# Two attention blocks on one core: a second Strassen step for four of the seven products of layer 0's second Q and K

## The chip, the cores and the metric

One NeuronCore of a Trainium2 chip runs the whole program. TensorE (PE) multiplies, VectorE (DVE) and ScalarE (ACT) empty its accumulators (PSUM banks) and do the element work, GpSimd (POOL) does a few small operations, and SyncE (SP) issues the DMAs. Each engine works through its own queue in order; semaphores join the queues. The metric is the device time of one execution in microseconds (us).

## The reference

x is 8 samples of 512 channels and 32x32 positions, float32 throughout. Two blocks follow each other, each with a residual. Cut to what matters, with C = 512 and N = 1024 positions:

```python
# layer 0, 8 heads of 64 channels
h = group_norm(x)                                  # 32 groups of 16 channels
q, k, v = split(qkv_w @ h + qkv_b)                 # three 512x512 products over N positions
o = softmax(q.T @ k / 8) applied to v, head by head
x = x + proj_w @ o + proj_b
# layer 1, one head over all channels, norm over the whole sample
n = norm(x)
q, k, v = wq @ n + bq, wk @ n + bk, wv @ n + bv
x = x + wo @ attention(q, k, v) + bo
```

## The kernel before

The kernel goes through the samples b = 0 to 7 one after the other. For one sample the stages are: layer 0's V (`make_v`, L517), its second Q and K (`pairs_qk` with oc = 1), the attention (64 units of scores, exponential and values), the first Q and K of the next sample (`pairs_qk` with oc = 0), the projection, and layer 1. "First" Q and K are output channels 0 to 127 and 256 to 383 (chunks 0 and 2), "second" are chunks 1 and 3. The attention goes through the chunks in the order 0, 2, 1, 3, so it begins with what the earlier stage has made.

Nearly all products are made by Strassen's scheme in Winograd's form (`strassen`, L410): both factors are cut into 2x2 quarters, and seven products A11 B11, A12 B21, S1 T1, S2 T2, S3 T3, A22 T4 and S4 B22 take the place of eight, where S1 to S4 and T1 to T4 are sums and differences of quarters. The weights' sums are made once by the first sample and stored in DRAM (`Weight`, L195); every later sample loads the finished set of seven parts (1792 KB) through SP. The sums T of the activations are made by VectorE (`Combined`, L378).

In the second Q and K, a quarter of the weight is 256 channels in by 128 out (parts of Q and of K apart), a quarter of the activations 256 channels by 512 positions. So one product is two matmuls (k = 0, 1) of 128x128 weights on 512 columns, four PE instructions in float32. Q and K are two `strassen` groups, and `together` (L454) lets them take turns. A group has two banks: `line`, in which A11 B11, S2 T2, S3 T3 and A22 T4 pile up, and `single` for the others. A bank may be written again only when ScalarE or VectorE has read it. ScalarE copies the line after its first three products (L421); VectorE adds a copy, the bias and a bank together (`done`, L511), and ScalarE writes the fourth quarter (L509).

`at_steps` (L466) walks through the steps of a stage and calls hooks between them. With PE, ACT and DVE the order in which the code calls is the order of their queues (`manual_schedule`); SP's order is found by the framework. In the second Q and K the hooks are: step 4 the mean of the next sample's group norm, step 5 its variance (small matmuls by `in_group`, L285, whose result VectorE takes, L289; GpSimd raises it to the power -0.5, L335; VectorE makes scale and shift, L342 to L344), steps 6 and 7 the normed x (L368 on ScalarE, L370 on VectorE), steps 8 and 9 the sums T for the next sample (L396) and the first two scores.

PSUM is one pool with two tags, "s" and "o", and two buffers of two banks for each. `room` (L278) gives the statistics a spare half of an "o" buffer when `strassen` has noted one in `spares`, and else a new "s" buffer. In the attention a unit is one chunk, one half of the queries and 128 keys: scores into an "s" buffer (L716), exponential by ScalarE (L645), a running sum of the exponentials by VectorE (L647), and values into an "o" buffer (L735). After a chunk's 16 units its running sums are folded by DMAs (`fold`, L824) and joined (L836). All tiles of 128x1024 in SBUF (x, q, k, v, exponentials, sums) come from one pool of 36 buffers, tag "t" (L88).

Layer 1 has a second Strassen step already: `halve_a` and `halve_b` (L1028, L1039) make the sums of a product's quarters, and `twice` (L1127) makes the product of 256 columns at a time in seven steps, with a line bank and a single bank.

Of the kernel before, what the change touches and what calls it, by code (L numbers as in the profile page):

```python
# [37 lines left out]
FP = mybir.dt.float32  # L38
AF = mybir.ActivationFunctionType
ALU = mybir.AluOpType  # L40
# [6 lines left out]
P = 128  # L47
# [4 lines left out]
HALF = 512  # L52
HD = 64
# [7 lines left out]
V_NW0, V_NB0, V_BQ0, V_BK0, V_BV0, V_BP0 = (NC * i for i in range(6))  # L61
# [4 lines left out]
def two_attention_blocks(  # L66
# [17 lines left out]
    nc = tc.nc  # L84
    B = x.shape[0]
# [4 lines left out]
    dram = ctx.enter_context(tc.tile_pool(name="dram", bufs=1, space=bass.MemoryType.DRAM))  # L90
# [47 lines left out]
    vec = const.tile([P, 12 * NC], FP, tag="vec", name="vec")  # L138
# [54 lines left out]
    stored = {}  # L193

    class Weight:  # L195
# [104 lines left out]
    class Norm:  # L300
# [54 lines left out]
        def bias(self):  # L355
            both, bias = self.tile("both"), self.tile("bias", NC)
            nc.vector.tensor_tensor(both, self.mean, self.rstd, ALU.mult)
            nc.vector.tensor_scalar(bias, made["v_g"], both, None, ALU.mult)
            nc.vector.tensor_tensor(bias, made["v_b"], bias, ALU.subtract)
            return bias  # L360
# [17 lines left out]
    class Combined:  # L378
# [5 lines left out]
        def take(self, quarters):  # L384
            (b11, self.b12), (b21, b22) = quarters
            for i in range(1, 5):
                self.parts[f"T{i}"] = tile2(f"t{i}_{self.name}")
            self.parts.update(B11=b11, B21=b21, B22=b22)
# [21 lines left out]
    def strassen(multiply, done, name, width=HALF, us=None, end=None):  # L410
# [36 lines left out]
            done(0, 1, single, us[2])  # L447
        yield

    def in_turn(*groups):  # L450
        for g in groups:
            yield from g

    def together(*groups):  # L454

        groups = list(groups)
        spares.clear()
        while groups:
            for g in list(groups):
                if next(g, g) is g:  # L460
                    groups.remove(g)
                else:
# [54 lines left out]
    def make_v(w, n2, bs, vs, name):  # L517


        def pairs(t):  # L520
            return t.rearrange("p (u o) -> p u o", u=2)

        def done(i, half, bank, u):
            v = vs[2 * half + n2][:, :, i * 2 * P : (i + 1) * 2 * P]
            if u is None:
                nc.scalar.copy(v, pairs(bank))
            else:
                nc.vector.tensor_tensor(v, pairs(bank), pairs(u), ALU.add)  # L528

        return strassen(by_positions(w, n2, bs), done, f"{name}_{n2}")  # L530
# [13 lines left out]
    class Rows:  # L544
# [33 lines left out]
        def add(self, i, name):  # L578

            t, c = const.tile([P, NC], FP, tag=name, name=name), self.columns[:, i]  # L580
            nc.vector.tensor_tensor(c[:, :2, :], c[:, :2, :], c[:, 2:, :], ALU.add)
            nc.vector.tensor_tensor(t, c[:, 0, :], c[:, 1, :], ALU.add)
            made[name] = t
            return t
# [90 lines left out]
    def flat(t):  # L675
        return t.rearrange("p h n -> p (h n)")

    def pairs_qk(w, oc, bs, qs, ks, b):

        for ts, n, bias, name in [(qs, 0, V_BQ0, "q"), (ks, 1, V_BK0, "k")]:  # L680
            for i in (oc, oc + 2):
                ts[i] = tile2(f"{name}_0_{b}_{i}")
            yield make_channels(
                w.parts[n], 0, oc, bs, vec[:, bias : bias + NC],
                lambda chunk, half, ts=ts: ts[chunk][:, half, :], f"{name}_0_{b}",
            )

    ORDER = [0, 2, 1, 3]

    def layer0(bs, qs, ks, b, norm_next):  # L690
# [3 lines left out]
        w = next_weight().parts[0]  # L694
        hooks = {}
        if norm_next is not None:
            for n in range(NC):
                hooks[n + 4] = [lambda cc=n, half=half: norm_next.of_half(cc, half) for half in range(2)]
            hooks[8] = [lambda cc=cc: norm_next.of_channels(cc) for cc in range(NC)]
        at_steps(together(*[make_v(w, n2, bs, vs, f"v_0_{b}") for n2 in range(2)]), hooks)  # L700
        vs = [vs[nt // 2][:, nt % 2, :] for nt in range(NT)]
        if b == 0:
            for rows in throughs:
# [4 lines left out]
        quarters = [(slice(i * HD, (i + 1) * HD), slice(j * HD, (j + 1) * HD), i, j)  # L708
                    for i in range(2) for j in range(2)]

        def scores(pair, g, kt):
            name = f"0_{b}_{pair}_{g}_{kt}"
            s = banks("s", f"s_{name}")
            for rows, cols, j, half in quarters:
                k0 = kt * P + half * HD
                nc.tensor.matmul(  # L716
                    s[cols, j, :], flat(ks[pair])[rows, k0 : k0 + HD],
                    qs[pair][rows, g, :], start=True, stop=True,
                )
            if kt == 1:  # L720
                first, accs[pair, g] = accs[pair, g], tile2(f"acc_{name}")
            else:
                first = accs.get((pair, g))
            p = exponentials(s, HD**-0.5, accs.get((pair, g)), first, name)
            if kt == 0:
                accs[pair, g] = p
            return p
# [35 lines left out]
        w = next_weight()  # L763
# [10 lines left out]
        hooks = {8: [lambda: score(0)], 9: [lambda: score(1)]}  # L774
# [9 lines left out]
        if b == 0:  # L784
            hooks.setdefault(7, []).append(p0.finish)
            hooks[8].insert(0, bias0)
        at_steps(together(*pairs_qk(w, 1, bs, qs, ks, b)), hooks)
        xs = load_x(b, nc.sync)
        norm = norm1(xs, b)

# [108 lines left out]
        for i in range(2, len(units) + 2):  # L899
# [6 lines left out]
            pair, g, kt = units[i - 5] if i >= 5 else (None, None, None)  # L906
# [92 lines left out]
    def attention1(xs, norm, b, at_values):  # L999
# [14 lines left out]
        bs = combine.parts  # L1014
# [1 line left out]

        twice_a, twice_b = {}, {}

        def halve(part, order):

            quarter = {}
            for i in range(2):
                for j in range(2):
                    k, n = order(i, j)
                    quarter[f"{i + 1}{j + 1}"] = part[:, k, n * 2 * P : (n + 1) * 2 * P]
            return quarter

        def halve_a(name):  # L1028
            q = {f"A{n}": v for n, v in halve(q_parts[name], lambda i, j: (j, i)).items()}
            t = flat(tile2(f"{name}_twice_{b}"))  # L1030
            q.update({f"S{n + 1}": t[:, n * 2 * P : (n + 1) * 2 * P] for n in range(4)})
            for n, x, y, op in [
                (1, "A21", "A22", ALU.add), (2, "S1", "A11", ALU.subtract),
                (3, "A11", "A21", ALU.subtract), (4, "A12", "S2", ALU.subtract),
            ]:
                nc.vector.tensor_tensor(q[f"S{n}"], q[x], q[y], op)
            twice_a[name] = q

        def halve_b(name):  # L1039
            q = {f"B{n}": v for n, v in halve(bs[name], lambda i, j: (i, j)).items()}  # L1040
            t = flat(tile2(f"{name}_twice_{b}"))
            q.update({f"T{n + 1}": t[:, n * 2 * P : (n + 1) * 2 * P] for n in range(4)})
            for n, x, y in [(1, "B12", "B11"), (2, "B22", "T1"), (3, "B22", "B12"), (4, "B21", "T2")]:
                nc.vector.tensor_tensor(q[f"T{n}"], q[x], q[y], ALU.subtract)
            twice_b[name] = q

        def make_q(c):
            def done(i, half, bank, u):
# [62 lines left out]
        def line(t):  # L1111


            bank = banks("s", f"ps_s_1_{b}_{t}")[:, 0, :]
            for a, v, to in [
                ("A11", "B11", ps[0][t // 2][0]), ("S2", "T2", ps[1][t // 2][0]),
                ("S3", "T3", ps[0][t // 2][1]),
            ]:
                for k in range(2):
                    nc.tensor.matmul(  # L1120
                        bank, bs[v][:, k, t * P : (t + 1) * P], q_parts[a][:, k, :],
                        start=a == "A11" and k == 0, stop=k == 1, skip_group_check=True,
                    )
                nc.scalar.copy(to[:, t % 2, :], bank)  # L1124
                yield
# [721 lines left out]
```

## Time and profile before

| | |
|---|---|
| median of 3 runs | 2872.4 us (2872.23 to 2872.4) |
| the profiled execution, its own time | 2871.3 us |
| its span, first to last instruction | 2869.6 us |
| granted TensorE clock | 1.0 |
| V of sample 3 (1119.66 to 1143.67) | 24.0 us; DVE busy 13.0, ACT 4.7 |
| second Q and K of sample 3, to the second scores (1143.67 to 1169.46) | 25.8 us |
| attention of sample 2 (816.6 to 926.9) | 110.3 us; PE busy throughout, DVE 86.7, ACT 70.2 |
| x, 512 KB a load, from issue to landing | 7.2 us (median of 92) |
| HBM read, written | 137.43 MB, 28.57 MB |

The profile page gives busy time by engine, the chain of work that ended last, and groups of instructions by source line. Timelines list instructions in order: start, duration, engine, line, operation, what is written from what, how many; in brackets the idle time before, and what ended it. PE's ends are modelled and overlap the next start, so the pace of PE is read from starts.

### The profile page before, as it was taken

How to read it: one execution, taken by the hardware profiler on the slowest of the kernel's cores; microseconds unless marked ns; L12 is line 12 of the kernel's file. 1: busy time of each engine (PE TensorE's matmuls, PEld its weight loads, DVE VectorE, ACT ScalarE, POOL GpSimd, SP SyncE). 2: the span in 40 equal slices, each digit the busy share in tenths (PEclk: the TensorE clock that was granted, in tenths of full speed). 3: DMA queues.
4: the chain of work that ended last, by engine and by line, in shares of the span. 5: the costliest groups of instructions: out<-in, count | busy, mean ns of one | idle time of the engine just before them, and what ended most of it. 6: DMA issues, size and time to landing. Idle time of an engine off the chain costs nothing.

```text
span 2869.6 us, 35809 instructions
## 1 busy us (share of the span) xinstructions
PE 2861.8 (100%) x14480; PEld 1436.3 (50%) x14480; DVE 1934.8 (67%) x2524; ACT 1110.3 (39%) x1536; POOL 109.5 (4%) x84
## 2 busy tenths in 40 slices
PE   9999999999999999999999999999999999999999
PEld 5434754347533475334653356533565335553365
DVE  5686576865757657676666766677665776647857
ACT  3462324623156231552315523165232652326432
POOL 0000000000000010000100001000010000100001
PEclk9999999999999999999999999999999999999999
DMA  8412122121222213212032120321203222122001
GB/s 272 162 41 73 52 95 92 42 74 52 95 92 49 75 43 110 82 45 92 26 121 73 44 91 26 121 78 46 84 26 121 78 56 78 38 80 68 8 1 38
DMA packets 77661, 210.87 MB, mean 73 GB/s; under 512 B 19888, under 2 KB 20656, under 8 KB 71088
## 3 DMA queue, kind: packets, MB, share of 16 engines
q1 hardware_dynamic: 77344, 208.48, 22.7%
q8 instruction: 115, 1.88, 0.3%
q14 instruction: 58, 0.48, 0.1%
q10 hardware_dynamic: 144, 0.02, 0.0%
HBM read 137.43 MB, written 28.57 MB: 58 GB/s over the span
## 4 chain that ended last, share of the span: by engine, by line
PE 98%; DVE 1%; SPq 0%; DMA 0%; issue 0%; ACT 0%; DVEq 0%; ACTq 0%
PE s L716 15%; PE ps_o L735 15%; PE ps_v L494 13%; PE ps_q L479 13%; PE ps_o L1244 13%; PE ps_k L479 7%; PE ps_p L479 6%; PE ps_s L1120 6%; PE ps_l L1136 4%; PE ps_s L1136 3%; PE ps_wvo L596 0%; PE ps_wqk L626 0%; DVE inv L658 0%; PE ps_o L1301 0%; DVE acc L647 0%; PE ps_sum L844 0%
## 5 line engine op out<-in xcount | busy, mean ns | idle before, releaser
L645 ACT ACTIVATE p<-s 128x1024 f32<-128x1024 f32 x512 | 523.9, 1025 | 322.2 <-PE s L716 310.5
L647 DVE TENSOR_TENSOR acc<-acc,p 128x1024 f32<-128x1024 f32 x384 | 469.0, 1221 | 103.4 <-ACT p L645 91.5
L716 PE MATMUL s<-q,k 64*64 64x512 f32 x4096 | 531.5, 590 | 0.0
L735 PE MATMUL ps_o<-p,v 64*64 64x512 f32 x4096 | 528.7, 589 | 0.0
L716 PEld LDWEIGHTS s<-q,k 64*64 64x64 f32 x4096 | 154.0, 133 | 288.9 <-issue 266.0
L735 PEld LDWEIGHTS ps_o<-p,v 64*64 64x64 f32 x4096 | 156.6, 133 | 282.8 <-issue 278.0
L528 DVE TENSOR_TENSOR v<-ps_v,u_v 128x512 f32<-128x512 f32 x96 | 66.2, 689 | 164.0 <-PE ps_v L494 111.4
L421 ACT COPY u_v<-ps_v 128x512 f32<-128x512 f32 x96 | 56.3, 586 | 303.5 <-PE ps_v L494 294.8
L1244 PE MATMUL ps_o<-t_p,s_v 128*128 128x512 f32 x384 | 168.2, 594 | 0.0
L421 ACT COPY u_q<-ps_q 128x512 f32<-128x512 f32 x96 | 55.9, 582 | 250.0 <-PE ps_q L479 250.0
L647 DVE TENSOR_TENSOR acc<-p,p 128x1024 f32<-128x1024 f32 x64 | 77.8, 1216 | 84.3 <-ACT p L645 84.3
L1146 DVE TENSOR_TENSOR p<-ps_l,p 128x512 f32<-128x512 f32 x104 | 71.1, 690 | 82.0 <-PE ps_l L1136 82.0
L1120 PE MATMUL ps_s<-s_q,t 128*128 128x512 f32 x256 | 120.3, 592 | 0.0
L1244 PEld LDWEIGHTS ps_o<-t_p,s_v 128*128 128x128 f32 x384 | 72.3, 190 | 94.5 <-issue 87.5
L1109 ACT ACTIVATE p<-p,factor 128x512 f32<-128x512 f32 (+1 forms) x112 | 86.8, 782 | 77.4 <-DVE p L1146 50.2
L479 PE MATMUL ps_q<-t,w_wqk 128*128 128x512 f32 x256 | 116.0, 597 | 0.0
L479 PE MATMUL ps_p<-t_p,w_p 128*128 128x512 f32 x256 | 114.3, 596 | 0.7 <-DVE inv L658 0.6
L494 PE MATMUL ps_v<-w_wvo,t 128*128 128x256 f32 x512 | 113.1, 379 | 0.0
L1244 PE MATMUL ps_o<-p,v 128*128 128x512 f32 x256 | 111.8, 594 | 0.1
L1146 DVE TENSOR_TENSOR p<-ps_s,p 128x512 f32<-128x512 f32 x88 | 60.7, 689 | 75.0 <-PE ps_s L1136 74.2
L856 DVE RECIPROCAL inv<-inv 128x512 f32<-128x512 f32 x28 | 93.7, 3346 | 22.9 <-ACT inv L654 22.9
L1124 ACT COPY p<-ps_s 128x512 f32<-128x512 f32 x96 | 56.1, 584 | 125.6 <-PE ps_s L1120 124.5
(320 smaller groups left out, 4083.9 us busy)
## 6 DMA issues: line engine op xcount, KB each, us to landing
x<-in_x SPq DMA_DIRECT2D x92, 512.0 KB, 7.2
w_qk<-stored_qk SPq DMA_DIRECT2D x14, 1792.0 KB, 7.2
inv<-inv SPq DMA_DIRECT2D x248, 64.0 KB, 2.0
w_wqk<-stored_wqk SPq DMA_DIRECT2D x8, 1792.0 KB, 8.1
fold<-acc SPq DMA_DIRECT2D x56, 256.0 KB, 3.1
w_wvo<-stored_wvo SPq DMA_DIRECT2D x8, 1792.0 KB, 7.7
out<-x SPq DMA_DIRECT2D x28, 512.0 KB, 2.8
w_v<-stored_v SPq DMA_DIRECT2D x7, 1792.0 KB, 7.1
```

The costliest lines, as they stand in the source:

```text
L421: nc.scalar.copy(us[n][:, :width], line[:, :width])
L479: nc.tensor.matmul(bank, w[a][:, k, c * P : (c + 1) * P], bs[b][:, k, :], start=fresh and k == 0, stop=k == 1, skip_group_check=True,)
L494: nc.tensor.matmul(bank[:, u * 2 * P : (u + 1) * 2 * P], bs[b][:, k, n * P : (n + 1) * P], w[a][:, k, :], start=fresh and u == k == 0, sto ...
L645: nc.scalar.activation(p, s, AF.Exp, scale=factor)
L647: nc.vector.tensor_tensor(acc, first, p, ALU.add)
L716: nc.tensor.matmul(s[cols, j, :], flat(ks[pair])[rows, k0 : k0 + HD], qs[pair][rows, g, :], start=True, stop=True,)
L735: nc.tensor.matmul(o[cols, half, :], vs[kt][rows, c0 : c0 + HD], p[rows, j, :], start=kt == 0, stop=kt == NT - 1,)
L856: nc.vector.reciprocal(invs[g], invs[g])
L1120: nc.tensor.matmul(bank, bs[v][:, k, t * P : (t + 1) * P], q_parts[a][:, k, :], start=a == "A11" and k == 0, stop=k == 1, skip_group_check ...
L1136: nc.tensor.matmul(bank[:, u * 2 * P : (u + 1) * 2 * P], v[y][:, u * P : (u + 1) * P], a[x], start=start and u == 0, stop=True, skip_group ...
L1146: nc.vector.tensor_tensor(at(r, t), bank, at(r, t), ALU.add)
L1244: nc.tensor.matmul(bank, v_parts[kt // 2][a][:, kt % 2, c * P : (c + 1) * P], p_parts[kt // 2][b][:, kt % 2, cols], start=fresh and kt == ...
```

## The change

Samples 1 to 7 make the second Q and K by `pairs_qk_twice`; sample 0 keeps `pairs_qk`. Q's and K's 128 output channels are now taken as the two block rows of one 256x256 weight. Four products (A12 B21, S1 T1, S4 B22, A22 T4) take a second step: each is cut again into 2x2 blocks, of 128x128 weights and 128 channels by 256 positions, and made as seven products of one matmul of 256 columns. Two of the four go together: their blocks lie side by side in one bank, are read by one instruction, and go to one tile (`c11` holds the first output half's C11 and C22, `c12` C12 and C21). `pair(0)` and `pair(1)` take turns over 14 steps; then `line(0)` for Q and `line(1)` for K make A11 B11, S2 T2 and S3 T3 in one step as before, over 6 steps, and VectorE adds the line and the bias into the tiles after each product. The hooks of steps 4 to 9 become those of steps 14 to 19.

The sums of the activations' quarters (T1 to T4 of B21, T1, B22 and T4) are made by VectorE in the first four steps of V: 16 subtractions of 128x256 a sample, into four new tiles. The sums of the weights' quarters (16 of 128x128) are made once, after the second scores of sample 0, and stored in DRAM (two stores of 512 KB); each later sample loads them (two loads) before its V, into two more tiles. q and k of these chunks now lie as halves in `c11` and `c12`, and the scores index them so. Layer 1's `halve_a` and `halve_b` call the new shared `sums_a` and `quarters_b`, and do what they did.

```diff
+    def sums_a(q, t):
+
+        n = t.shape[1] // 4
+        q.update({f"S{i + 1}": t[:, i * n : (i + 1) * n] for i in range(4)})
+        for i, x, y, op in [
+            (1, "A21", "A22", ALU.add), (2, "S1", "A11", ALU.subtract),
+            (3, "A11", "A21", ALU.subtract), (4, "A12", "S2", ALU.subtract),
+        ]:
+            nc.vector.tensor_tensor(q[f"S{i}"], q[x], q[y], op)
+        return q
...
+    def quarters_b(part, name):
+
+        q = {f"B{n}": v for n, v in halve(part, lambda i, j: (i, j)).items()}
+        t = flat(tile2(name))
+        q.update({f"T{n + 1}": t[:, n * 2 * P : (n + 1) * 2 * P] for n in range(4)})
+        for n, x, y in [(1, "B12", "B11"), (2, "B22", "T1"), (3, "B22", "B12"), (4, "B21", "T2")]:
+            nc.vector.tensor_tensor(q[f"T{n}"], q[x], q[y], ALU.subtract)
+        return q
...
+    PAIRS = [[("A12", "B21"), ("S1", "T1")], [("S4", "B22"), ("A22", "T4")]]
+
+    class WeightTwice:
...
+        def __init__(self, name, make=None):
+            tiles = [flat(tile2(f"{name}_twice_{n}")) for n in range(2)]
+            key, self.tiles = f"{name}_twice", tiles
+            if make is None:
+                nc.sync.dma_start(tiles[0], stored[key][:, : 8 * P])
+                nc.sync.dma_start(tiles[1], stored[key][:, 8 * P :])
+                return
+            for n, pair in enumerate(PAIRS):
+                for i, (a, _) in enumerate(pair):
+                    sums_a(self.quarters(a, make), tiles[n][:, i * 4 * P : (i + 1) * 4 * P])
+            stored[key] = dram.tile([P, 16 * P], FP, tag=key, name=f"stored_{key}")
+            for n in range(2):
+                nc.sync.dma_start(stored[key][:, n * 8 * P : (n + 1) * 8 * P], tiles[n])
...
+    def by_two_steps(rows_of, twice_a, bs, twice_b, pairs, bias, name):
+
+        def pair(n):
+            line, single = (banks(tag, f"ps_{tag}{n}_{name}")[:, 0, :] for tag in "so")
+
+            def multiply(bank, x, y, start):
+                for i, (a, v) in enumerate(PAIRS[n]):
+                    nc.tensor.matmul(
+                        bank[:, i * 2 * P : (i + 1) * 2 * P], twice_a[a][x], twice_b[v][y],
+                        start=start and i == 0, stop=True, skip_group_check=True,
+                    )
+
+            def at(r, t):
+                return pairs[n][r][:, :, t * 2 * P : (t + 1) * 2 * P]
+
+            def of(bank):
+                return bank.rearrange("p (i q) -> p i q", i=2)
+
+            def add(bank, r, t):
+                nc.vector.tensor_tensor(at(r, t), of(bank), at(r, t), ALU.add)
+
+            def take(bank, r, t):
+                nc.scalar.copy(at(r, t), of(bank))
+
+            for bank, x, y, start, use, r, t in [
+                (line, "A11", "B11", True, take, 0, 0), (single, "A12", "B21", True, add, 0, 0),
+                (line, "S2", "T2", False, take, 0, 1), (single, "S1", "T1", True, take, 1, 1),
+                (line, "S3", "T3", False, add, 1, 1), (single, "S4", "B22", False, add, 0, 1),
+                (line, "A22", "T4", False, take, 1, 0),
+            ]:
+                multiply(bank, x, y, start)
+                use(bank, r, t)
+                yield
+
+        def line(i):
+            bank = banks("o", f"ps_l{i}_{name}")[:, 0, :]
+
+            def multiply(a, v, start):
+                for k in range(2):
+                    nc.tensor.matmul(
+                        bank, rows_of(i, a)[:, k, :], bs[v][:, k, :], start=start and k == 0,
+                        stop=k == 1, skip_group_check=True,
+                    )
+
+            def add(j, half, n):
+                c = pairs[j][i][:, half, :]
+                nc.vector.scalar_tensor_tensor(c, bank, bias(i, n), c, ALU.add, ALU.add)
+
+            (c11, c22), (c12, _) = ([p[i][:, half, :] for half in range(2)] for p in pairs)
+            nc.vector.tensor_tensor(c12, c12, c22, ALU.add)
+            multiply("A11", "B11", True)
+            add(0, 0, 0)
+            yield
+            multiply("S2", "T2", False)
+            add(1, 0, 0)
+            yield
+            multiply("S3", "T3", False)
+            add(0, 1, 1)
+            add(1, 1, 1)
+            yield
+
+        yield from together(pair(0), pair(1))
+        yield from together(line(0), line(1))
...
+    def pairs_qk_twice(w, twice_a, oc, bs, twice_b, qs, ks, b):
+
+        pairs = [[tile2(f"{n}_{name}_0_{b}_{oc}") for name in "qk"] for n in ["c11", "c12"]]
+        for i, ts in enumerate([qs, ks]):
+            (c11, c22), (c12, c21) = ([p[i][:, half, :] for half in range(2)] for p in pairs)
+            ts[oc], ts[oc + 2] = [c11, c12], [c21, c22]
+
+        def bias(i, n):
+            at = [V_BQ0, V_BK0][i] + oc + 2 * n
+            return vec[:, at : at + 1]
+
+        of = both_of(w)
+        return by_two_steps(of, twice_a.all(of), bs, twice_b, pairs, bias, f"qk_0_{b}")
...
+        twice_b = {}
+        if b > 0:
+            twice_a = WeightTwice("qk13")
+            for n, part in enumerate(["B21", "T1", "B22", "T4"]):
+                hooks.setdefault(n, []).append(lambda part=part: twice_b.update(
+                    {part: quarters_b(bs[part], f"{part}_twice_0_{b}")}
+                ))
...
-                    s[cols, j, :], flat(ks[pair])[rows, k0 : k0 + HD],
-                    qs[pair][rows, g, :], start=True, stop=True,
+                    s[cols, j, :], ks[pair][k0 // HALF][rows, k0 % HALF : k0 % HALF + HD],
+                    qs[pair][g][rows, :], start=True, stop=True,
...
-        at_steps(together(*pairs_qk(w, 1, bs, qs, ks, b)), hooks)
+        if b == 0:
+            hooks[9].append(lambda: WeightTwice("qk13", both_of(w)))
+            at_steps(together(*pairs_qk(w, 1, bs, qs, ks, b)), hooks)
+        else:
+            hooks = {n + 10: more for n, more in hooks.items()}
+            at_steps(pairs_qk_twice(w, twice_a, 1, bs, twice_b, qs, ks, b), hooks)
```

More of the change, by code (lines that the diff above doesn't have):

```diff
@@ L448, in strassen, with halve @@
         yield
+    def halve(part, order):
+        quarter = {}
+        for i in range(2):
+            for j in range(2):
+                k, n = order(i, j)
+                quarter[f"{i + 1}{j + 1}"] = part[:, k, n * 2 * P : (n + 1) * 2 * P]
+        return quarter
+    def sums_a(q, t):
[7 more added lines that the diff above has]
+        return q
@@ new lines, in two_attention_blocks, with quarters, all @@
+    class WeightTwice:
[12 more added lines that the diff above has]
+                nc.sync.dma_start(stored[key][:, n * 8 * P : (n + 1) * 8 * P], tiles[n])
+        def quarters(self, a, rows_of):
+            return {f"A{i + 1}{j + 1}": rows_of(i, a)[:, j, :] for i in range(2) for j in range(2)}
+        def all(self, rows_of):
+            made = {}
+            for n, pair in enumerate(PAIRS):
+                for i, (a, _) in enumerate(pair):
+                    q, t = self.quarters(a, rows_of), self.tiles[n][:, i * 4 * P : (i + 1) * 4 * P]
+                    q.update({f"S{m + 1}": t[:, m * P : (m + 1) * P] for m in range(4)})
+                    made[a] = q
+            return made
@@ L681, in pairs_qk, with both_of @@
             for i in (oc, oc + 2):
-                ts[i] = tile2(f"{name}_0_{b}_{i}")
+                t = tile2(f"{name}_0_{b}_{i}")
+                ts[i] = [t[:, half, :] for half in range(2)]
             yield make_channels(
                 w.parts[n], 0, oc, bs, vec[:, bias : bias + NC],
-                lambda chunk, half, ts=ts: ts[chunk][:, half, :], f"{name}_0_{b}",
+                lambda chunk, half, ts=ts: ts[chunk][half], f"{name}_0_{b}",
             )
+    def both_of(w):
+        return lambda i, name: w.parts[i][name]
+    def pairs_qk_twice(w, twice_a, oc, bs, twice_b, qs, ks, b):
[8 more added lines that the diff above has]
+        return by_two_steps(of, twice_a.all(of), bs, twice_b, pairs, bias, f"qk_0_{b}")
     ORDER = [0, 2, 1, 3]
@@ L1017, in attention1 @@
         twice_a, twice_b = {}, {}
[L1019 to L1026, printed above, removed]
         def halve_a(name):
             q = {f"A{n}": v for n, v in halve(q_parts[name], lambda i, j: (j, i)).items()}
[L1030 to L1037, printed above, removed]
-        def halve_b(name):
[L1040 to L1045, printed above, removed]
+            twice_a[name] = sums_a(q, flat(tile2(f"{name}_twice_{b}")))
+        def halve_b(name):
+            twice_b[name] = quarters_b(bs[name], f"{name}_twice_{b}")
         def make_q(c):
```

## The prediction

> **What bounds the kernel now.** I read the page first: busy time by engine, then the chain that ended last.
>
> ```profile
> span 2869.6 us, 35809 instructions
> ...
> PE 2861.8 (100%) x14480; PEld 1436.3 (50%) x14480; DVE 1934.8 (67%) x2524; ACT 1110.3 (39%) x1536; POOL 109.5 (4%) x84
> ...
> PE 98%; DVE 1%; SPq 0%; DMA 0%; issue 0%; ACT 0%; DVEq 0%; ACTq 0%
> ```
>
> TensorE has work in 2861.8 of 2869.6 us, and the chain runs along it for 98% of the span. So what leaves PE's stream leaves the span, unless a new wait takes its place. The second view is the timeline of sample 3's second Q and K, PE alone.
>
> ```profile
> 1141.94 1.89 PE L494 MATMUL ps_v<-w_v,x 128*128 128x256 f32 x8
> 1143.67 3.60 PE L479 MATMUL ps_q<-x,w_qk 128*128 128x512 f32 x8
> 1147.10 3.60 PE L479 MATMUL ps_k<-x,w_qk 128*128 128x512 f32 x8
> 1150.54 1.88 PE L479 MATMUL ps_q<-t_again,w_qk 128*128 128x512 f32 x4
> ...
> 1155.68 0.28 PE L285 MATMUL ps_q<-stat,in_group 128*128 128x4 f32 x2
> 1155.83 1.96 PE L479 MATMUL ps_k<-t_again,w_qk 128*128 128x512 f32 x4
> 1157.62 0.28 PE L285 MATMUL ps_q<-spread,in_group 128*128 128x4 f32 x2
> ...
> 1164.81 1.09 PE L716 MATMUL s<-q,k 64*64 64x512 f32 x8
> ...
> 1169.46 1.95 PE L716 MATMUL s<-q,k 64*64 64x512 f32 x16
> ```
>
> Rows overlap because ends are modelled, so I price by starts. 1147.10 - 1143.67 is 3.43 us for 8 instructions: 0.429 us for one of 512 columns, 1.717 for a product (four). The V row's 8 instructions of 256 columns take 1143.67 - 1141.94 = 1.73: 0.216 each. Each pair of statistics matmuls adds 1157.62 - 1155.68 - 1.717 = 0.22. There is no idle time from 1143.67 to the second scores at 1169.46: 25.79 us.
>
> The third view is VectorE in the same stretch, because the change gives VectorE more to do there.
>
> ```profile
> 1156.60 0.16 DVE L329 TENSOR_TENSOR spread<-spread,stat 128x4 f32<-128x4 f32 x1
> 1157.94 0.16 DVE L289 COPY mean_v<-ps_q 128x4 f32<-128x4 f32 x1 [1.19 <-PE ps_q L285]
> 1158.14 0.17 DVE L334 TENSOR_SCALAR rstd<-mean_v 128x4 f32<-128x4 f32 x1
> 1159.44 0.16 DVE L342 TENSOR_TENSOR scale<-rstd,vec 128x4 f32<-128x4 f32 x1 [1.14 <-POOL rstd L335]
> 1159.84 0.16 DVE L344 TENSOR_TENSOR shift<-vec,shift 128x4 f32<-128x4 f32 x1
> 1160.38 0.75 DVE L511 SCALAR_TENSOR_TENSOR q<-ps_q,vec,u_q 128x512 f32<-128x512 f32 x1 [0.38 <-ACT u_q L421]
> 1161.05 0.99 DVE L370 TENSOR_SCALAR x<-x,scale,shift 128x512 f32<-128x512 f32 x2
> ```
>
> VectorE works in order, and stands still 1.14 us for GpSimd's power. Whatever stands behind it waits too.
>
> **What is removed and added on PE**, in samples 1 to 7. Removed: 28 matmuls of 512 columns, 56 instructions, 56 x 0.429 = 24.03 us. Added: `pair(0)` and `pair(1)`, 14 steps of two matmuls of 256 columns, 56 x 0.216 = 12.08; `line(0)` and `line(1)`, 6 products, 24 x 0.429 = 10.30. Together 22.38: 1.65 us less a sample, 7 x 1.65 = 11.55. Sample 0 keeps the old way.
>
> The Trainium skill (TensorE: Matmul & The Clock Gate, Back-to-back issue gap) speaks against smaller matmuls: spacing in a stream is set by weight load and matmul together, and the plain formula counts too little at small N (81 ns where it gives 56, at N = 128). If each of the 56 took 25 ns more, as there, 1.4 of the 1.65 us would go, and the sum below would come to some 2872.8. The V row above, with the same shape and a weight load for each, has its 0.216 with the load inside, so I keep the row.
>
> **Hand-overs in the pairs.** A step lasts 0.863 us and ends with one drain: a ScalarE copy (0.586, the `u_q` row L421 has 582 ns) or a VectorE add (0.69). Layer 1 already does the same in `twice`:
>
> ```profile
> 1064.79 1.03 PE L1136 MATMUL ps_l<-S_twice,B_twice 128*128 128x256 f32 x4
> 1065.66 1.03 PE L1136 MATMUL ps_l<-A_twice,T_twice 128*128 128x256 f32 x4
> ...
> 1065.86 0.69 DVE L1146 TENSOR_TENSOR p<-ps_l,p 128x512 f32<-128x512 f32 x1 [0.17 <-PE ps_l L1136]
> 1066.72 0.69 DVE L1146 TENSOR_TENSOR p<-ps_l,p 128x512 f32<-128x512 f32 x1 [0.17 <-PE ps_l L1136]
> ```
>
> Steps start 0.87 apart and a drain 0.2 after its product, all on VectorE, without a gap on PE. A bank is written again three steps (2.59 us) after its product ended, or later; drain and way back need 0.2 + 0.69 + 0.25 = 1.14. `line(0)` at step 14 takes the bank of step 10: same room. I price the pairs' waits at 0; the gap-free row excludes a loss per step, and if the cover went, each step could cost up to 1.14, 16 us a sample.
>
> **Sums for the second step.** 16 subtractions of 128x256 at 0.417 us (the `B_twice` and `T_twice` rows of layer 1, 416 to 421 ns) are 6.7 us of VectorE in the V stage. There VectorE is busy 13.0 of 24.0 us. PE could meet them in one place: the second sample half's `S1 T1` (8.6 us into V) needs the V add queued behind four of them. That add waits for its own product until 7.2 anyway and ends at 7.9; then twelve more end at 12.9, the statistics at 15.4, and the next V add comes at 16.2 as now. Price 0; uncovered, 6.7 a sample.
>
> **Loads.** Two issues of 512 KB each stand on SP behind the four x loads (issued 1122.46 to 1124.85). Statistics of the first and the third x load began on landing, at 1128.41 and 1131.16, so one lands every 1.4 us, and the two new ones by about 1137. PE needs them at step 4, 1143.67 + 3.45 = 1147.1: 10 us of room. Behind them on SP is the projection's weight, which waits for V's end (1143.86) in any case. In sample 0, 16 sums of 128x128 (between the 0.16 of a 128x4 row and 0.417; I take 0.28, nearer 256 columns by the step from 417 to 685 ns: 4.5 us, ends 2.6 and 6.7) run on VectorE at the start of the attention, and two stores stand on SP before three of the residual's x loads, which the projection needs some 140 us later. Price 0; uncovered, 4.5 once.
>
> **The wait that is new**, and the only one I price. The hooks of steps 4 to 9 move to 14 to 19, so the statistics meet the lines' adds (0.745 each) in one VectorE queue, and take "s" buffers, which ScalarE's last copies free at 12.0 and 12.9, in time. From the stage's start: `line(0)` A11 12.09 to 13.80, statistics to 14.02, `line(1)` A11 to 15.74. VectorE: first add 14.07 to 14.82, mean and spread to 15.50 (0.20 a step), in time for the second statistics at 15.74; then C12's sum of K (0.69) and the add of `line(1)`, to 16.80; variance copy, rstd to 17.12, GpSimd, scale and shift to 18.81 (1.69 from rstd's end, as 1158.31 to 1160.00 above). Only then the add after `line(0)` S2, to 19.50. PE has ended `line(1)` S2 at 19.39 and needs that add for `line(0)` S3: with 0.25 for the way back (a weight load's 0.19 and an assumed 0.06 for the semaphore) it stands 0.35 us. Late next is normed x, then the scores, for which PE does not wait on VectorE. If all of VectorE's operations follow at their full length plus 0.08 (as 1156.60 after 1156.40 + 0.16) and not overlapped (1161.05 starts before 1161.13), the add ends at 20.34 and the stand is 1.2 to 1.3; if GpSimd ends early, 0. Sample 7 has no next norm: 0.
>
> **Sum.** 6 x (1.65 - 0.35) + 1.65 = 9.45 us. Against the profiled span: 2869.6 - 9.45 = 2860.15; the median of the runs lies 2.8 above that span, so **2863.0**. Ends: 11.55 gives 2860.9, 6 x 0.35 + 1.65 = 3.75 gives 2868.7.
>
> **Rivals.**
> *The wait for the variance takes most of it.* At the long end above, 1.3 us in each of six samples, the time is 2868.7, no difference that can be told (0.2%, 5.7 us, is about what a measurement of this kernel can tell from none). For it: the 1.14 us stand of VectorE, and ten more VectorE operations in the stage. Against: the queue's rows overlap rather than spread.
> *VectorE's arrears reach PE in the attention: slower.* In my walk the last combination for the next sample ends at 29.3, the second exponential at 26.6; now both meet (1172.50). So the running sums start 2.7 us late. If buffers or sums handed that on to PE, 7 x 2.7 = 18.9 against 9.45 won: 2881.9; it decides from 1.35 us a sample. For it: VectorE is busy 86.7 of the attention's 110.3 us, and the exponentials already waited 9.7 us in all for folded sums (L836). Against: each unit lasts 1.72 and the sum's row 1.30, so the arrears are gone in 7 of the 64 units, and the first folding comes at unit 17.
> *Nothing lost: the full 11.55*, 2860.9, if the power's chain starts a little earlier; part of the forecast's own range.
>
> **How the numbers follow.** Forecast (gain of 5.7 to 11.6) 0.75; the variance's wait 0.16, between 0 and 5.7 won; arrears 0.09. Time 2863.0, the forecast's own range 2860.5 to 2866.7, widened to 2868.5 to take in most of the first rival. Faster 0.75, same 0.16, slower 0.09.
>
> **What would show it.** In the changed trace, second Q and K: 56 instructions of 256 columns 0.216 apart without gaps; first matmul to second scores 24.5 instead of 25.8 us; an idle PE of some 0.35 before `line(0)` S3, ended by VectorE's add; statistics and V as before; the first running sum 2 to 3 us after its exponential, caught up by unit 8. Wrong would be: gaps between the pair steps, PE waiting for a landing of the stored sums, V longer than 24.2 us, or a unit of the attention over 1.72 on average.

## The result and the profile after

| | before | after |
|---|---|---|
| median of 7 runs each, in turns on one chip | 2872.06 us (2871.66 to 2872.4) | 2862.0 us (2860.76 to 2863.07) |
| ratio | | 0.9964, interval 0.9953 to 0.9976 |
| the profiled execution, its span | 2871.3, 2869.6 | 2861.29, 2859.6 |

The change makes the kernel faster by 10.06 us. 2863.0 was forecast, with 2860.5 to 2868.5 for the range. The page of the changed kernel, busy time by engine and the chain that ended last:

```profile
span 2859.6 us, 36447 instructions
...
PE 2852.0 (100%) x14648; PEld 1468.0 (51%) x14648; DVE 2020.6 (71%) x2722; ACT 1110.3 (39%) x1536; POOL 109.5 (4%) x84
...
PE 98%; DVE 1%; SPq 0%; DMA 0%; issue 0%; ACT 0%; POOL 0%; DVEq 0%; POOLq 0%
```

PE's busy time falls by 9.8 us (2861.8 to 2852.0) while its instructions grow by 168: in each of seven samples 56 of 512 columns go, and 56 of 256 columns and 24 of 512 come. The 85.8 us that VectorE has to do in addition (1934.8 to 2020.6) do not show on the chain.

The second Q and K of sample 3, PE's timeline of the changed kernel (start, duration, engine, line, operation, what is written from what, how many):

```profile
1141.56 0.59 PE L524 MATMUL ps_s_qk<-x,w_qk 128*128 128x256 f32 x2
1141.99 0.59 PE L524 MATMUL ps_s_qk<-t_again,w_qk 128*128 128x256 f32 x2
...
1145.01 0.59 PE L524 MATMUL ps_s_qk<-B_twice,qk_twice 128*128 128x256 f32 x2
...
1153.64 1.88 PE L556 MATMUL ps_l_qk<-x,w_qk 128*128 128x512 f32 x4
1155.36 0.28 PE L285 MATMUL ps_m<-stat,in_group 128*128 128x4 f32 x2
...
1157.44 5.48 PE L556 MATMUL ps_l_qk<-t_again,w_qk 128*128 128x512 f32 x12
1162.85 1.09 PE L872 MATMUL s<-q,k 64*64 64x512 f32 x8
1163.87 1.98 PE L556 MATMUL ps_l_qk<-t_again,w_qk 128*128 128x512 f32 x4
1165.78 1.52 PE L872 MATMUL s<-q,k 64*64 64x512 f32 x12
```

By starts, the 56 instructions of the two pairs take 1153.64 - 1141.56 = 12.08 us, 0.2157 each, with no stand between them, and the stage to the second scores 1165.78 - 1141.56 = 24.22 in place of 25.79. The third row is the first to read the stored sums `qk_twice`: it follows its forerunner (1144.58) at the pace of the others.

To see where the rest went I cut both traces into stages by PE's starts and subtracted. Equal to 0.01 us in every sample: V (24.17 from its first matmul), the attention of samples 0 to 6 after its second scores (110.35), the next first Q and K (25.35), layer 1 of samples 0 to 6 (142.95). What differs:

| | before | after | gain |
|---|---|---|---|
| second Q and K, samples 1 to 6, each | 25.79 | 24.22 | 6 x 1.57 |
| second Q and K, sample 7 | 25.34 | 23.69 | 1.65 |
| projection to layer 1's first Q, samples 0 to 6 in all | 170.15 | 170.52 | -0.37 |
| the same stage, sample 7 | 26.18 | 26.11 | 0.07 |
| start of sample 0's V (the first loads) | 59.65 | 60.46 | -0.81 |
| layer 1's first Q of sample 7 to the span's end | 148.94 | 148.87 | 0.07 |

9.42 + 1.65 - 0.37 + 0.07 - 0.81 + 0.07 = 10.03, the spans' 10.0. The change does not touch the last four rows. The start scatters: in the ten traces of the changed kernel and of the nine made from it, it lies between 59.43 and 60.57.

VectorE in the same stretch of the changed kernel, and at the start of its attention:

```profile
1158.36 0.17 DVE L334 TENSOR_SCALAR rstd<-mean_v 128x4 f32<-128x4 f32 x1
1159.66 0.16 DVE L342 TENSOR_TENSOR scale<-rstd,vec 128x4 f32<-128x4 f32 x1 [1.14 <-POOL rstd L335]
1159.86 0.16 DVE L343 TENSOR_TENSOR shift<-mean_m,scale 128x4 f32<-128x4 f32 x1
1160.06 0.16 DVE L344 TENSOR_TENSOR shift<-vec,shift 128x4 f32<-128x4 f32 x1
1160.13 0.74 DVE L563 SCALAR_TENSOR_TENSOR c_q<-ps_l_qk,vec,c_q 128x512 f32<-128x512 f32 x1
...
1170.64 1.22 DVE L778 TENSOR_TENSOR acc<-p,p 128x1024 f32<-128x1024 f32 x1
```

The queue stands 1.14 us for GpSimd's power, and the add that PE needs for `line(0)` S3 comes out at 1160.13 + 0.74 = 1160.87. PE's weight loads show what that does:

```profile
1160.10 0.19 PEld L556 LDWEIGHTS ps_l_qk<-t_again,w_qk 128*128 128x128 f32 x1 [0.24 <-issue]
1160.93 0.30 PEld L556 LDWEIGHTS ps_l_qk<-t_again,w_qk 128*128 128x128 f32 x2 [0.64 <-DVE c_q L563]
```

The usual stand before a weight load is 0.24; here it is 0.64, ended by that add, so the load is 0.40 late. Loads run ahead of their matmuls by one instruction (0.43), and so PE's matmuls show no stand at all in the timeline above. Only the starts of two of them lie 0.51 apart in place of 0.43 (1160.96 and 1161.47): the 1.65 - 1.57 = 0.08 that the stage gains less here than in sample 7, which has no next norm.

### The profile page after: what moved, and what is told of

It reads as the page before. It is cut to its first block, busy times and chain, and to the rows that moved or that the text cites. A ratio compares the mean times of both kernels' runs of the same rounds, so it can differ in the third digit from the quotient of the medians.

```text
span 2859.6 us, 36447 instructions
## 1 busy us (share of the span) xinstructions
PE 2852.0 (100%) x14648; PEld 1468.0 (51%) x14648; DVE 2020.6 (71%) x2722; ACT 1110.3 (39%) x1536; POOL 109.5 (4%) x84
## 4 chain that ended last, share of the span: by engine, by line
PE 98%; DVE 1%; SPq 0%; DMA 0%; issue 0%; ACT 0%; POOL 0%; DVEq 0%; POOLq 0%
PE s L872 16%; PE ps_o L891 15%; PE ps_v L625 14%; PE ps_o L1384 13%; PE ps_q L610 10%; PE ps_p L610 6%; PE ps_s L1260 6%; PE ps_l L1276 4%; PE ps_k L610 3%; PE ps_s L1276 3%; PE ps_l_qk L556 3%; PE ps_s_qk L524 2%; PE ps_o_qk L524 1%; PE ps_wvo L727 1%; PE ps_wqk L757 0%; PE ps_o L1441 0%
## 5 line engine op out<-in xcount | busy, mean ns | idle before, releaser
L872 PE MATMUL s<-q,k 64*64 64x512 f32 x2304 | 298.5, 591 | 0.0
L872 PE MATMUL s<-c_q,c_k 64*64 64x512 f32 x1792 | 233.0, 590 | 0.0
L872 PEld LDWEIGHTS s<-q,k 64*64 64x64 f32 x2304 | 86.3, 133 | 162.6 <-issue 156.6
L872 PEld LDWEIGHTS s<-c_q,c_k 64*64 64x64 f32 x1792 | 67.7, 133 | 126.3 <-issue 114.9
L778 DVE TENSOR_TENSOR acc<-p,p 128x1024 f32<-128x1024 f32 x64 | 77.8, 1216 | 73.9 <-ACT p L776 73.9
L421 ACT COPY u_q<-ps_q 128x512 f32<-128x512 f32 x75 | 43.6, 581 | 177.1 <-PE ps_q L610 177.1
```

What stands on the lines that cost most here:

```text
L421: nc.scalar.copy(us[n][:, :width], line[:, :width])
L778: nc.vector.tensor_tensor(acc, first, p, ALU.add)
L872: nc.tensor.matmul(s[cols, j, :], ks[pair][k0 // HALF][rows, k0 % HALF : k0 % HALF + HD], qs[pair][g][rows, :], start=True, stop=True,)
```

## The experiments

Each stretch named below runs from the second Q and K's first matmul to the second scores, unless it says otherwise. Times are medians, ratios are to runs of the kernel before beside them, whose medians lay between 2871.90 and 2872.25.

**Four matmuls of 256 columns issued twice.** If the columns are the whole gain, putting their time back should take it away.

```
-  nc.tensor.matmul(
-      bank[:, i * 2 * P : (i + 1) * 2 * P], twice_a[a][x], twice_b[v][y], ...
+  for _ in range(2 if (x, y) in (("A11", "B11"), ("A12", "B21")) and i == 0 else 1):
+      nc.tensor.matmul(
+          bank[:, i * 2 * P : (i + 1) * 2 * P], twice_a[a][x], twice_b[v][y], ...
```

> The changed kernel, with four matmuls of 256 columns issued twice in each second Q and K of samples 1 to 7 (the first of A11 B11 and of A12 B21 in both pairs): 4 x 256 columns, what the second step saves. The result is unchanged, and every drain, hook and wait stays where it is. Columns theory: 4 x 0.432 = 1.73 us a sample come back, so the stretch from the first matmul to the second scores goes from 24.22 to 25.95 us and the time from 2862.0 to about 2874. Rival (the gain comes from the new order of drains and hooks, not from columns): the added matmuls are partly hidden in waits, and the time stays under 2868.

Measured: 2874.33 (2873.28 to 2874.76), ratio to before 1.0008 (0.9999 to 1.0017). The stretch is 25.95, 1.73 more than in the changed kernel: eight instructions at 0.216. The gain is columns, and a small matmul costs its 0.216 here and no more.

**The second step in samples 4 to 7 only.**

```
-  if b > 0:
+  if b > 3:
...
-  if b == 0:
-      hooks[9].append(lambda: WeightTwice("qk13", both_of(w)))
+  if b < 4:
+      if b == 0:
+          hooks[9].append(lambda: WeightTwice("qk13", both_of(w)))
```

> The second step in samples 4 to 7 alone; samples 1 to 3 make the second Q and K as before. If the gain is one of each sample (1.57 in samples 1 to 6, 1.65 in sample 7 by the traces), 3 x 1.57 + 1.65 = 6.4 us of it are left: 2865.7. If it comes from something done once (the start, the first sample, the lie of the buffers), the time is 2862 or 2872.

Measured: 2866.25 (2865.12 to 2866.91), 0.9981 (0.9972 to 0.9990). Samples 1 to 3 take 25.79, 4 to 6 take 24.22, 7 takes 23.69. So the gain belongs to the samples, and the sums that sample 0 makes and stores, which stay in this kernel, take nothing that the trace shows.

**Every quarter sum of the activations made twice**, 32 subtractions in V in place of 16: the cover of the sums, which the prediction priced at 0.

```
-  hooks.setdefault(n, []).append(lambda part=part: twice_b.update(
+  hooks.setdefault(n, []).extend([lambda part=part: twice_b.update(
...
-  ))
+  )] * 2)
```

> The changed kernel, with the sums of the activations' quarters made twice over in the V stage (32 subtractions of 128x256 a sample in place of 16; the second set goes to further tiles and is the one used). By the walk of V's VectorE queue with the measured 0.385 us for one: the second V add ends 9.0 us into V, where PE wants it at 8.6, and the third set of adds comes at 20.6 to 21.3, where PE wants the bank at 19.0: PE stands some 2.4 us a sample in samples 1 to 6 and 0.4 in sample 7, V lasts 26.6 in place of 24.17 us, the time is about 2877. Rival (VectorE has room for more): V stays at 24.17, 2862.

Measured: 2871.39 (2870.92 to 2873.45), 0.9999 (0.9989 to 1.0008): the gain is gone. V takes 25.97 in samples 1 to 6, 1.80 longer where 2.4 was expected, and 0.40 longer in sample 7, as expected. PE and VectorE of this kernel in sample 3:

```profile
1140.33 1.99 PE L625 MATMUL ps_v<-w_v,x 128*128 128x256 f32 x8 [1.14 <-DVE v L659]
```

```profile
1137.22 2.46 DVE L314 BATCH_NORM_STATS2 part<-x 128x6 f32<-128x512 f32 x4
1139.60 0.67 DVE L659 TENSOR_TENSOR v<-ps_v,u_v 128x512 f32<-128x512 f32 x1
```

PE stands for the V add, and the add stands behind four statistics, which stand behind the doubled sums. In sample 7 there are no statistics, and only 0.40 is left. What covers the 16 sums is the time in which VectorE has nothing to do in V; with twice the work it is used up.

**The stored sums loaded only at the end of V**, in place of its first third.

```
-  nc.sync.dma_start(tiles[0], stored[key][:, : 8 * P])
-  nc.sync.dma_start(tiles[1], stored[key][:, 8 * P :])
...
+  def load_late(self):
+      for n in range(2):
+          nc.vector.tensor_copy(self.tiles[n][:, :NC], vec[:, :NC])
+          nc.sync.dma_start(self.tiles[n], stored["qk13_twice"][:, n * 8 * P : (n + 1) * 8 * P])
...
+  hooks[9] = [twice_a.load_late]
```

> The changed kernel, with the two loads of the stored weight sums held back to the end of V, each by a small VectorE copy into its tile (128x4), so that they are issued about 1 us into the second Q and K, behind the projection's weight (1792 KB). PE wants them 3.45 us into the stage. If the 10 us of room counted in the prediction were cover, PE now stands 5 to 7 us a sample at step 4: 35 to 49 us, 2897 to 2911. Rival (such loads land within 3 us): 2862 to 2865.

Measured: 2915.41 (2914.29 to 2916.97), 1.0152 (1.0136 to 1.0167): 6.9 to 8.7 us more in a stretch, and the time lies above the 2897 to 2911 that were expected. PE of this kernel in sample 3, then the stretches of time around it (from:to and its length, busy time of PE, weight loads, DVE, ACT and POOL with instructions, then PE's granted clock, DMA share, GB/s):

```profile
1166.69 1.19 PE L529 MATMUL ps_s_qk<-B_twice,qk_twice 128*128 128x256 f32 x2 [5.42 <-DMA qk_twice<-stored_qk_twice]
1167.67 1.06 PE L529 MATMUL ps_s_qk<-T_twice,qk_twice 128*128 128x256 f32 x2
```

```profile
1150.00:1161.00 11.00, 11.00 (x53) 9.57 (x51) 5.85 (x15) 2.93 (x5) 0.00 (x0) 1.00 0.21 60
1167.00:1169.60 2.60, 2.60 (x7) 2.06 (x7) 0.00 (x0) 0.59 (x1) 0.00 (x0) 0.50 0.01 3
1170.00:1175.00 5.00, 5.00 (x25) 4.41 (x24) 1.94 (x3) 1.76 (x3) 0.00 (x0) 1.00 0.00 2
```

The first load is issued at 1158.64, behind the projection's weight, and lands at 1166.55. The stand for it is 5.42 us here and 5.15 to 5.53 in the seven samples, inside the 5 to 7 that were expected. What was not: after it PE runs at a granted clock of 0.50 until some 1169.6, at twice its usual spacing (0.86 for two instructions), which adds some 1.5. In other samples the half clock lasts up to 6.1 us: the seven stands are 37.3 us in all, and the 30.0 us at half clock behind them cost 15.0, together 52.3 of the 53.4 by which this kernel is slower than the changed one. In the changed kernel the same two loads of sample 3 land at 1132.43 and 1133.68, and PE reads them first at 1145.01: 11 us of room, where the prediction counted 10.

**VectorE held up at the start of the attention**, by four and by sixteen more combinations of 1.22 us after the second scores, in samples 1 to 6: the rival of the arrears, the work that VectorE is behind with there.

```
+  if norm_next is not None:
+      hooks[19] += [lambda: combine.make(4)] * 4
```

The other kernel has 16 in place of 4.

> The changed kernel, with the last combination for the next sample (128x1024, 1.22 us) done four times more on VectorE after the second scores, in samples 1 to 6: the same values are written again. VectorE's arrears at the start of the attention go from some 1.8 to 6.7 us. If a unit leaves VectorE 0.4 us free, they are gone by unit 17 and PE's pace in the attention stays as it is (110.34 us from the second scores to the next Q and K): 2862. Rival (arrears reach PE): up to 4.9 us a sample more, 2862 to 2891.

> As the run with four extra combinations, with 16 (18 us more on VectorE after the second scores, samples 1 to 6). At 0.42 us free in a unit the arrears of some 20 us would last 47 of the 64 units. The first bank of the values is wanted again at unit 18, and VectorE's add that frees it comes about then: PE stands for 1 to 6 us a sample, 2868 to 2898. If all of it were handed on: 6 x 18, 2970. If arrears never reach PE: 2862.

With four: 2861.36 (2860.0 to 2861.39), 0.9964 (0.9950 to 0.9977), as the changed kernel, and PE's attention is 110.34 as before. With sixteen: 2916.94 (2916.09 to 2917.9), 1.0157 (1.0142 to 1.0173), 8.4 to 10 us more in a sample, above the expected 1 to 6. The rows of sample 3 in the second of these kernels: VectorE, ScalarE and PE.

```profile
1188.50 20.11 DVE L396 TENSOR_TENSOR t<-x,t 128x1024 f32<-128x1024 f32 x16
1208.53 7.86 DVE L778 TENSOR_TENSOR acc<-acc,p 128x1024 f32<-128x1024 f32 x6
```

```profile
1200.02 1.03 ACT L776 ACTIVATE p<-s 128x1024 f32<-128x1024 f32 x1 [0.75 <-PE s L872]
1209.84 1.02 ACT L776 ACTIVATE p<-s 128x1024 f32<-128x1024 f32 x1 [8.79 <-DVE acc L778]
```

```profile
1210.91 1.98 PE L872 MATMUL s<-q,k 64*64 64x512 f32 x8 [6.73 <-ACT p L776]
1212.68 1.93 PE L891 MATMUL ps_o<-p,v 64*64 64x512 f32 x8
```

The way from VectorE to PE is seen here: sums that are 20 us late leave the exponentials in their buffers, ScalarE finds none for the next, and then PE has no bank to write scores to. Until then PE keeps its pace: exponentials went on for 11.5 us after VectorE turned to the extra work. Then the same half clock as above: between 1211 and 1216 the granted clock is 0.50, and eight instructions start 1.71 apart in place of 0.86. PE's stands sum to 40.4 us in six samples, and the half clock lasts 27.7 us behind them, which costs 13.8: together 54.2 of the 54.9 by which the kernel is slower than the changed one. The rival of the arrears is a real mechanism, but it decides somewhere between 4 and 16 such operations more than the changed kernel has.

**The statistics' small matmuls earlier**, so that GpSimd's power is out of the way of the lines' adds. First at steps 4 and 5, in the spare halves of the single banks:

```
-  line, single = (banks(tag, f"ps_{tag}{n}_{name}")[:, 0, :] for tag in "so")
+  line, single = (banks(tag, f"ps_{tag}{n}_{name}") for tag in "so")
+  spares.append(single[:, 1, :])
+  line, single = line[:, 0, :], single[:, 0, :]
...
-  hooks = {n + 10: more for n, more in hooks.items()}
+  hooks = {n + (10 if n > 5 else 0): more for n, more in hooks.items()}
```

> The changed kernel, with the mean and variance back at steps 4 and 5 (in spare halves of the pairs' single banks), away from the adds of the lines. My walk of the VectorE queue put 0.35 us of waiting per sample on that meeting; the trace of the changed kernel shows only some 0.08 (the second matmul of line 0's third product starts 0.94 after the first, not 0.86). By the trace: 6 x 0.08 = 0.5 us less, 2861.5, which can't be told from 2862.0, a stretch of 24.14 us, and the first running sum earlier. By the walk: 2 us less, 2860. By the rival of the prediction (1.3 us a sample): 2854.

Measured: 2864.49 (2862.96 to 2866.1), 0.9974 (0.9964 to 0.9984): the stretch is 24.70, 0.48 longer, where it should have been 0.08 shorter. PE's weight loads in sample 3 of this kernel:

```profile
1147.23 0.30 PEld L285 LDWEIGHTS ps_o_qk<-spread,in_group 128*128 128x128 f32 x2 [0.28 <-DVE spread L329]
1147.87 0.30 PEld L526 LDWEIGHTS ps_o_qk<-B_twice,qk_twice 128*128 128x128 f32 x2 [0.34 <-DVE mean_v L289]
```

A step of a pair lasts 0.86. From the mean's matmul (1146.11) over the chain on VectorE (mean_m starts at 1146.42, the last spread ends at 1147.17) to the variance's weight load (1147.23) it takes 1.12, so the chain does not fit into a step. The variance's matmul waits for the spread, and the next step's matmul waits for VectorE to read the variance out of the buffer that both share. The lines themselves run without a late load here.

Then at steps 8 and 11, in the second pair's spare half; and, for a look at the jitter of the projection's stage, the second reciprocal of the next Q and K at step 5 instead of 6:

```
+  if n:
+      spares.append(single[:, 1, :])
...
-  hooks = {n + 10: more for n, more in hooks.items()}
+  hooks = {{4: 8, 5: 11}.get(n, n + 10): more for n, more in hooks.items()}
...
-  5: [lambda: held_couple(0)],
-  6: [lambda: one_over_couple(couple, 1)],
+  5: [lambda: held_couple(0), lambda: one_over_couple(couple, 1)],
```

> A version meant to beat both kernels: mean and variance at steps 8 and 11 of the pairs, three steps apart (in a spare half of the second pair's single bank), and in the first Q and K of the next sample the second reciprocal one step earlier (step 5, not 6), so that its DMAs land before the projection wants them. If the waits are the ones that the traces show (0.08 us a sample in the lines; 0 to 0.35 at the projection's second pair of products, where VectorE waits for the landing), some 0.5 to 1 us less than the changed kernel's 2862.0, and less spread. If the earlier reciprocal holds up the adds of Q and K, more than 2862.

Measured: 2865.13 (2864.37 to 2866.09), 0.9976 (0.9966 to 0.9985). The stretch is 1.05 longer in samples 1 to 6. PE of this kernel in sample 3:

```profile
1153.97 0.39 PE L285 MATMUL ps_o_qk<-spread,in_group 128*128 128x4 f32 x2 [0.78 <-DVE c_q L539]
```

Now the spread is there in time, but the variance's matmul waits until VectorE has taken the product out of the other half of the same buffer. Both placements lose to the changed kernel's: its separate banks cost it 0.08 a sample, and these two, which share a buffer with the pairs, take 0.48 and 1.05 more than it (the first in part because the chain does not fit into a step). But the projection's stage, 24.26 to 24.62 in the changed kernel's samples 0 to 6, is 24.03 in six of the seven here.

**The changed kernel with the earlier reciprocal alone** (the last three lines of the diff above).

> The changed kernel with one callback moved: the second reciprocal of a couple, which ends in a load of 1/sum that VectorE's divide waits for at the start of the projection, is issued one product earlier in the next sample's Q and K (step 5 instead of 6). Theory: in the changed kernel that load lands too late, so that the stretch from the projection's first matmul to layer 1's first Q takes 24.26 to 24.62 us in samples 0 to 6 where 24.03 would do; the experiment with moved statistics had 24.03 in six of its seven samples after the same step. Expected: 24.03 in nearly all samples, 2.0 to 2.5 us less in all, about 2859.5 to 2860 us in the median, and everything else as in the changed kernel. Rival: the 24.03 belonged to the other layout of that experiment (another phase of the DMA queue); then the stretch stays at 24.26 to 24.62 and the time at 2862.

Measured: 2859.17 (2858.26 to 2859.8), 0.9954 (0.9940 to 0.9967): below every run of the changed kernel. The projection's stage is 24.03 in six samples and 24.69 in one (sample 4), in all 1.65 less. VectorE at the start of the projection of sample 3, first the changed kernel, then this one:

```profile
1304.25 0.69 DVE L911 TENSOR_TENSOR o<-o,inv 128x512 f32<-128x512 f32 x1 [1.22 <-DMA inv<-inv]
1304.86 0.68 DVE L961 TENSOR_TENSOR t_p<-o,o 128x512 f32<-128x512 f32 x1
...
1309.51 0.67 DVE L1134 TENSOR_TENSOR u_p<-ps_p,u_p 128x512 f32<-128x512 f32 x1
```

```profile
1302.57 0.69 DVE L911 TENSOR_TENSOR o<-o,inv 128x512 f32<-128x512 f32 x1 [0.50 <-DMA inv<-inv]
1303.18 0.68 DVE L961 TENSOR_TENSOR t_p<-o,o 128x512 f32<-128x512 f32 x1
...
1307.83 0.67 DVE L1133 TENSOR_TENSOR u_p<-ps_p,u_p 128x512 f32<-128x512 f32 x1
```

And a weight load in the changed kernel that stands 0.83 instead of 0.24 for that add:

```profile
1310.23 0.30 PEld L610 LDWEIGHTS ps_p<-t_p,w_p 128*128 128x128 f32 x2 [0.83 <-DVE u_p L1134]
```

VectorE's last divide waits for a DMA of 1/sum to land, the sums for the projection and its first adds queue behind it, and PE meets the second of these adds too late. One product earlier, the landing is waited for 0.50 instead of 1.22, and PE has no late load there. In sample 4 VectorE still waits 1.60: three of the sixteen loads before it took 3.1 to 3.6 us to land in place of some 2.0, and why is not shown. The wait is in no way the change's own work: the kernel before has the same one (1.21 in sample 3; the stage 24.24 to 24.46).

## Why the prediction was right, point by point

- **PE's columns, 1.65 us a sample.** Right: 1.65 in sample 7, where nothing else is in the way, 0.216 for each of 56 without gaps, and 0.216 again for each of eight given back. The estimate that it was weighed against carried the 25 ns that the Trainium skill has at N = 128 (TensorE: Matmul & The Clock Gate, Back-to-back issue gap) over to these float32 matmuls of 256 columns: the loss of some 1.4 us a sample that it would have made was not there.
- **The pairs' hand-overs, 0.** Right; no stand in 12.08 us.
- **Sums in V, 0.** Right: V is 24.17 in both kernels. The sums end at 1129.64 in sample 3, 12.3 us into V (a start at 1117.38), where the walk had 12.9. The margin is less than their own 6.7 us: doubled, they cost 1.80.
- **Loads and stores, 0.** Right; only held to the end of V do the loads cost 5.15 to 5.53 a sample, and what the clock adds. The 16 sums of 128x128 in sample 0, put at 0.28 each, last 0.281 to 0.293.
- **The wait for the variance, 0.35 in each of six samples.** The mechanism was right, with the releaser that was named, and its size was not: 0.08. This is the term that was mis-sized, 2.1 us in the sum against 0.5. The add ended 19.31 us into the stage (1160.87 - 1141.56) where the walk had 19.50, since VectorE's operations start before the one ahead has ended (the add at 1160.13, after a row of 0.16 that began at 1160.06). And the way back was priced as a load in PE's path, 0.25; the loads run 0.43 ahead of their matmuls, and of 0.40 late 0.08 came through.
- **The first rival, 1.3 a sample,** falls with it. The walk's long end, of operations that neither overlap nor shorten, is not how the queue runs.
- **The second rival, the arrears.** They were there: the first running sum starts at 1170.64, 2.7 us after the second exponential's end (1166.94 + 1.02 = 1167.96), as walked. But the prediction misread the kernel before, where it let both meet at 1172.50: there the second exponential ends at 1171.64, so the sum was already 0.9 late, and the change adds only 1.8. PE did not feel the arrears, nor 4.9 us more. Twenty more it did. The two exponentials, before and after:

```profile
1170.61 1.03 ACT L645 ACTIVATE p<-s 128x1024 f32<-128x1024 f32 x1 [2.08 <-PE s L716]
```

```profile
1166.94 1.02 ACT L776 ACTIVATE p<-s 128x1024 f32<-128x1024 f32 x1 [1.91 <-PE s L872]
```

- **The sum.** 9.45 was forecast and 10.06 measured. In the trace the stage gave 11.07, the prediction's "nothing lost" less 0.5; the first loads and the projection's stage took 1.0 back, and both scatter among the traces of these kernels. So part of the closeness is luck: two misses, 1.6 and 1.0 us, have opposite signs.

## What to carry to other kernels

Where one engine has no idle time, price a change by its instructions at the pace of a row of the same shape, and go through the other engines' queues only for who is behind whom: here that gave the columns' part of the gain to 0.01 us a sample and named the one wait, though at over four times its size. Weight loads run ahead of their matmuls (0.43 us here), and a hand-over that made one of them 0.40 late cost PE 0.08; loads 0.20 and 0.59 late in sample 3's projection cost 0.27. So price lateness against that lead and not from the add's end. And before giving a small result a spare half of a bank, look at who writes and reads the other half: the two placements that shared a buffer lost 0.5 and 1.05 us a sample against one that cost 0.08.

## What the hardware showed that I had not expected

After PE had stood for 5.15 to 6.73 us, thirteen times in two experiments, the granted clock was 0.50 for the next 2.9 to 6.1 us, and then 1.0 again. After shorter stands, up to 1.74 us (the projection of sample 3 with the statistics at steps 4 and 5), it stayed at 1.0. The length of the stand does not set the way back: it is 3.1 us after a stand of 5.15 and 6.0 after one of 5.23. Nor does the clock fall after one fixed time: in the trace it goes to 0.50 between 2.2 and 4.9 us after the (modelled) end of PE's last matmul. The Trainium skill (TensorE: Matmul & The Clock Gate, What's actually happening) says that PE falls to half rate after at least one idle window of some 3.4 us and comes back after at least one busy one; these rows agree in kind, though both times can be shorter than 3.4, and no run here has a stand between 1.8 and 5.1 us.

VectorE's operations can start before the one ahead has ended, where they need nothing from it: in V of the changed kernel's sample 3 a quarter sum of 0.42 us is followed after 0.34 by one that doesn't read it (1123.09, 1123.43), and after 0.45 by one that does (1122.64, 1123.09).
